# Graph attention on one core: sums per head on their own partitions, one copy a batch, PSUM operands for VectorE, more tiles gathered before the table, more rows fetched one by one, and a last batch in two parts

## The chip, the cores and the metric

The kernel runs on one core of a Trainium2 chip. The metric is the device time of one launch in microseconds (us), the median of three runs. Beside the runs stands one profiled execution, from which all rows of the trace come. Engines are named as in the profile: PE (TensorE), PEld (its weight loads), DVE (VectorE), ACT (ScalarE), POOL (GpSimd) and SP (SyncE, which here only starts DMAs). A letter q behind an engine (SPq, ACTq) is its queue of DMA issues and waits.

## The reference

12,500 nodes with 128 features, 412,500 edges sorted by their target. For each edge an attention value is made from the source row, the target row and 64 edge features; a softmax over the edges of a target (with a maximum that is at least 0, and a denominator that also counts the edges that do not go to this target) weighs the source rows, which are summed per target and added to x.

```python
h = relu(layernorm(x));  h = (h @ W_node.T).reshape(N, 4, 32);  e = (edge_attr @ W_edge.T).reshape(E, 4, 32)
att = sum(concat([h[src], h[tgt], e]) * a)             # per edge and head
att = where(att > 0, att, 0.2 * att)
m = maximum(segment_max(att, tgt), 0)
ex = exp(att - m[tgt])
denom = segment_sum(ex, tgt) + (E - deg) * exp(-m)
out = x + segment_sum(ex / denom[tgt] * h[src], tgt)   # summed over edges of a target
```

## The kernel before

**Preparation (to about 150 us).** 98 blocks of 128 nodes are normalised, projected by `wall` (128x144: per head 32 features, two ones and the source part of the attention; behind them four target parts) and written to a table in HBM (rows of 576 bytes). While that goes on, POOL gathers the source rows of the first edges from `x` itself, since the table is not there yet: these are the "raw" tiles, `RAW = (49, 9)`, all 49 of batch 0 and 9 of batch 1. They are normalised and projected in the same loop, three tiles a unit, behind the table's units. In the same loop the ranges of the targets are worked out (`chunk_ranges`), and ACT clears the accumulator `acc` in one copy (L453).

**Batches.** Edges go in tiles of 128, seven tiles a chunk (896 edges), seven chunks a batch (49 tiles), 66 batches; the last has six chunks, the last chunk three tiles. For each tile POOL issues an indirect DMA (L632) that gathers 128 rows of the table into `hs`, a ring of three buffers. From batch 5 on, the first tile of a batch (the first two where the batch number divides by `EVERY` = 4, none in the last batch) is not gathered by POOL but fetched row by row with DMAs of 576 bytes from the queues of SP (96 an iteration, or all that is left) and ACT (64): `by_row`, `row_by_row`, L658.

The order is written out by hand; engines run their own instructions in that order, and wait for each other by semaphores. Iteration b of the main loop holds: the loads of the next batches on SP (indices, the near target values `lw`, edge features `eft`, rows, penalties `pen`); `gather` of batch b+1 on POOL, behind a small memset `gate` (L627) that waits until the sums of batch b-2 have read the buffer; then on DVE `weigh(b)`, `mark(b)`, `scatter(b)`, the merge of the batches before (`close`), and `choose(b+1)`; on PE the sums of `scatter(b)` and then the edge part `z` of batch b+2 (`begin`, L691).

- `weigh` (L734 to L760): waits for the batch's rows, adds source and target parts, transposes to 32 partitions x 896, adds `z`, applies the slope 0.2 (L742, one instruction, both inputs the SBUF tile `att`), scans forward and back for the segment maximum (L745, L748), subtracts, and ACT takes the exponent (L752) while DVE makes four products of `pen` and `m` (L756).
- `mark` (L702 to L710): the 0/1 matrix `hot` (edge x 32 target slots).
- `scatter` (L774, L781): each chunk is multiplied with its weights (DVE, seven steps), and PE sums four chunks at a time: 128x128 stationary (four chunks' `hot` side by side), 502 columns moving, so the sums of a head land on the partitions of the chunk and not on those of the head. `collect` (L823) therefore copies 28 blocks of 32x35 a batch on ACT to where the merge wants them. The last batch takes `scatter_few` (L796: 128x32 stationary, 140 columns).
- `merge` (L829 to L869): two batches at a time (the last four singly) are joined by scans over chunks and added to `acc`, one iteration later. `finish` (L940 to L967) divides and stores a part of the nodes; inside the loop ACT moves its 16 blocks (L955), at the very end PE does (L957, 128x32 stationary at four column positions in turn).
- The last batch's rows are waited for in two steps (tiles 0 to 4, then 5 and 6): the steps up to the forward scan are done twice, everything behind it once for the whole batch, after the merge of the batch before.

Of the kernel before, what the change touches and what calls it, by code (L numbers as in the profile page):

```python
# [18 lines left out]
P = 128  # L19
N = 12500  # L20
D = 128
# [19 lines left out]
G = 4  # L41
RING = 3
AHEAD = 4
EARLY = 5
# [4 lines left out]
LOOSE = 4  # L49
RAW = (T * CB, XB)  # L50
# [7 lines left out]
SPLIT = 2 * AW  # L58
RUN = (G - 1) * ROW + SPLIT
# [9 lines left out]
SPROWS = 96  # L69
ACTROWS = 64  # L70
EVERY = 4
# [18 lines left out]
def by_row(b):  # L90

    return (2 if b % EVERY == 0 else 1) if LOOSE < b < NBT - 1 else 0
# [39 lines left out]
def kernel(  # L132
# [40 lines left out]
    acc = const.tile([P, NQ, AW], F32, name="acc")  # L173

# [6 lines left out]
    row_at = shared[P // 2:P // 2 + NBT - 3, :2 * P]  # L181
# [45 lines left out]
    with (  # L227
# [42 lines left out]
        wall = p1.tile([P, ROW], F32, name="wall")  # L270
# [34 lines left out]
        def load_rows(b0, n):  # L305
# [3 lines left out]
            if s.raw:  # L309
                k = int(b0 >= NB + RAW[0])  # L310
                i = b0 - NB - k * RAW[0]
                s.rows = raw[k][:, i:i + n, :]
# [99 lines left out]
        sizes += [min(XB, n - i) for n in RAW for i in range(0, n, XB)]  # L412
# [39 lines left out]
        def chunk_ranges():  # L452
            nc.scalar.copy(acc.rearrange("p q d -> p (q d)"), carry_m.to_broadcast([P, NQ * AW]))  # L453
# [260 lines left out]
    def weigh(s, before):  # L714
# [7 lines left out]
        zst = work.tile([P, T, R], F32, name="zst")  # L722
        att = work.tile([P, BUF], F32, name="a")[:R, :CE]
        up = ps.tile([P, BANKS * 512], F32, name="up")[:R, :CE]
        own = s.hs[:, :, :EROW].rearrange("p (t q) (h k) -> p t q h k", t=T, h=H)[:, :, :s.chunks, :, AW - 1]

        def grouped(what, g):
            return what.rearrange("r (t g i) -> r g t i", g=NQT, i=R)[:, g, :, :]

        for t0, t1 in ((0, EARLY), (EARLY, T)) if s.b == NBT - 1 else ((0, T),):  # L730
            if t0:
                landed(nc.vector, "late", late_sems, late_done, 0, s.hs[:, EARLY * CB:, :], s.ends[:, :, :, :])
            e0, e1 = t0 * P, t1 * P
            nc.vector.tensor_tensor(logits[:, t0:t1, :s.chunks * H].rearrange("p t (q h) -> p t q h", h=H),  # L734
                                    own[:, t0:t1], pick[:, t0:t1, :s.chunks, :H], op=OP.add)
            nc.vector.transpose(zst[:, t0:t1, :].rearrange("p t i -> p (t i)"),
                                logits[:, t0:t1, :].rearrange("p t i -> p (t i)"))
            for g in range(NQT):
                on_half(s, nc.vector.tensor_tensor(grouped(att, g)[:, t0:t1, :], grouped(s.z, g)[:, t0:t1, :],  # L739
                                                   zst[g * R:(g + 1) * R, t0:t1, :], op=OP.add))  # L740
            z = s.z[:, e0:e1]
            on_half(s, nc.vector.scalar_tensor_tensor(z, att[:, e0:e1], 0.2, att[:, e0:e1], op0=OP.mult, op1=OP.max))  # L742
            if before:
                collect(before, 0)
            on_half(s, nc.vector.tensor_tensor_scan(up[:, e0:e1], s.pen[:, e0:e1], z, up[:, e0 - 1:e0] if e0 else 0.0,  # L745
                                                    op0=OP.add, op1=OP.max))
        m = work.tile([P, BUF], F32, name="m")[:R, :CE]
        nc.vector.tensor_tensor_scan(m[:, ::-1], s.pen[:, CE:0:-1], up[:, ::-1], 0.0, op0=OP.add, op1=OP.max)  # L748
        on_half(s, nc.vector.tensor_tensor(att, s.z, m, op=OP.subtract))  # L749
        both = work.tile([P, 2, T, R], F32, name="both")  # L750
        for g in range(NQT):
            nc.scalar.activation(both[g * R:(g + 1) * R, 0, :, :], grouped(att, g), AF.Exp)  # L752
        if before:
            collect(before, 1)
# [576 lines left out]
```

## Time and profile before

| what | us |
|---|---|
| runs | 4022.22, 4022.31, 4023.95 (median 4022.31) |
| profiled execution | 4021.72, its span 4019.9 |
| POOL busy | 3010.7 (75%) |
| DVE busy | 2373.7 (59%) |
| PE busy | 1455.8 (36%) |
| ACT busy | 865.9 (22%) |

How to read it: the share of busy time says little by itself, since POOL's gathers are short instructions with a fixed pause between them that the page counts as idle time "issue" and not as work. The view of the groups by line gives busy time, the mean of one instruction, and what ended the idle time before them; the view of one line gives minimum, median and maximum; the timeline gives start and length of each instruction (several alike in a row are joined, "x28"), and in brackets the idle time before it. fp32 matmuls stand as two records each.

### The profile page before, as it was taken

The page shows a single profiled execution, that of the slowest core. Times are in us where ns is not written, and L with a number is a line of the kernel's source. Part 1 is how long each engine was busy: PE and PEld are TensorE (multiplying, and loading weights), DVE is VectorE, ACT ScalarE, POOL GpSimd, SP SyncE. Part 2 cuts the span into 40 slices and gives each one's busy share as a digit, 9 for nine tenths or more (in the row PEclk, how much of TensorE's full clock was granted, in tenths as well). Part 3 has the DMA queues.
Part 4 walks back from the last instruction along what each step waited for, and adds up shares of the span by engine and source line. Part 5 has one row for each costly group of instructions (what it writes and reads, how often), then busy time and mean ns, then how long its engine had stood idle before and what let it go on. Part 6 is the DMA issues. An engine that isn't in the chain of part 4 may idle for free.

```text
span 4019.9 us, 40260 instructions
## 1 busy us (share of the span) xinstructions
PE 1455.8 (36%) x3485; PEld 570.9 (14%) x3485; DVE 2373.7 (59%) x4282; ACT 865.9 (22%) x2682; POOL 3010.7 (75%) x3224
## 2 busy tenths in 40 slices
PE   5652432432442442442342442342342342343342
PEld 4320110110110110110110111110111110111111
DVE  7895565565565565465565565566465456465466
ACT  6321122112122112112122112122122122122122
POOL 6777777777777777777777777777777777777774
PEclk9776666766666666666666766676776676676676
DMA  7443333433333433433433433433334333434331
GB/s 214 130 134 109 100 96 108 110 89 99 107 91 108 110 94 99 110 87 105 109 97 95 110 88 106 108 104 88 110 89 110 104 108 85 109 89 109 109 93 42
DMA packets 283438, 418.03 MB, mean 104 GB/s; under 512 B 81019, under 2 KB 199862, under 8 KB 283146
## 3 DMA queue, kind: packets, MB, share of 16 engines
q0 software_dynamic: 100736, 231.80, 22.4%
q1 hardware_dynamic: 161232, 173.91, 14.5%
q10 hardware_dynamic: 21178, 9.69, 1.0%
q14 instruction: 262, 2.15, 0.2%
q8 instruction: 30, 0.49, 0.1%
HBM read 399.60 MB, written 15.51 MB: 103 GB/s over the span
## 4 chain that ended last, share of the span: by engine, by line
POOL 66%; issue 22%; DVE 7%; PE 3%; DMA 1%; ACT 1%; POOLq 0%; DVEq 0%; SPq 0%; ACTq 0%
POOL hs L632 66%; PE pa L781 1%; DVE hs L774 1%; PE z L691 1%; DVE stats L335 1%; DMA hs<-table,ends 1%; DVE hT L381 1%; DVE pick L607 1%; DVE m L748 0%; DVE up L745 0%; DVE hot L710 0%; DVE a L739 0%; ACT both L752 0%; DVE z L742 0%; DVE a L749 0%
## 5 line engine op out<-in xcount | busy, mean ns | idle before, releaser
L632 POOL DMA_INDIRECT hs<-table,ends x3090 | 2946.6, 954 | 945.0 <-issue 933.4
L781 PE MATMUL pa<-hs,hot 128*128 128x502 f32 x1820 | 924.6, 672 | 2428.0 <-DVE hs L774 2428.0
L734 DVE TENSOR_TENSOR logits<-hs,pick 128x196 f32<-128x196 f32 (+1 forms) x67 | 32.9, 491 | 1349.4 <-DVEq L666 1349.2
L781 PEld LDWEIGHTS pa<-hs,hot 128*128 128x128 f32 x1820 | 395.8, 222 | 2948.9 <-issue 2892.3
L823 ACT COPY r<-pa 32x35 f32<-32x35 f32 x1820 | 379.7, 209 | 1531.0 <-issue 1204.4
L774 DVE TENSOR_TENSOR hs<-hs,exr 128x924 f32<-128x924 f32 x455 | 472.5, 1110 | 0.0
L691 PE MATMUL z<-eft,wa 128*32 128x512 f32 (+3 forms) x1056 | 436.5, 549 | 13.5 <-DMA eft<-in_ef 13.5
L752 ACT ACTIVATE both<-a 32x224 f32<-32x224 f32 x264 | 102.4, 388 | 1153.1 <-DVE a L749 1150.7
L607 DVE COPY_PREDICATED pick<-exr,lw 128x3136 f32<-128x3136 int32 x66 | 239.8, 3633 | 0.0
L607 DVE COPY_PREDICATED pick<-exr,pick 128x1568 f32<-128x1568 int32 (+3 forms) x198 | 230.6, 1165 | 6.8
L590 ACT COPY pick<-lw 128x3136 f32<-128x3136 f32 x66 | 184.8, 2800 | 2.7 <-ACTq L666 1.2
L869 DVE TENSOR_TENSOR acc<-acc,a 128x70 f32 x461 | 107.2, 233 | 70.0 <-issue 51.2
L691 PEld LDWEIGHTS z<-eft,wa 128*32 128x32 f32 (+1 forms) x1056 | 94.6, 109 | 358.0 <-issue 350.7
L745 DVE TENSOR_TENSOR_SCAN up<-pen_sb,z 32x896 f32<-32x896 f32 x66 | 132.6, 2010 | 2.3
L748 DVE TENSOR_TENSOR_SCAN m<-pen_sb,up 32x896 f32<-32x896 f32 x66 | 132.5, 2007 | 2.3
L710 DVE TENSOR_TENSOR hot<-exr,key 128x448 f32<-128x448 f32 (+1 forms) x260 | 129.0, 559 | 6.7
L739 DVE TENSOR_TENSOR a<-z,zst 32x224 f32<-32x224 f32 (+2 forms) x268 | 101.0, 377 | 12.6 <-PE z L691 2.7
L756 DVE SCALAR_TENSOR_TENSOR both<-pen_sb,m 32x224 f32<-32x224 f32 x264 | 100.2, 380 | 2.7
L955 ACT COPY up<-a 32x224 f32<-32x224 f32 (+1 forms) x224 | 74.5, 332 | 36.0 <-DVE a L947 29.3
L742 DVE SCALAR_TENSOR_TENSOR z<-a 32x896 f32<-32x896 f32 (+1 forms) x67 | 72.1, 1076 | 2.3
L749 DVE TENSOR_TENSOR a<-z,m 32x896 f32<-32x896 f32 x66 | 71.3, 1080 | 2.3
L239 POOL DMA_INDIRECT hs<-in_x,ends x58 | 54.9, 947 | 18.1 <-issue 17.4
(166 smaller groups left out, 991.3 us busy)
## 6 DMA issues: line engine op xcount, KB each, us to landing
hs<-table SPq DMA_DIRECT2D x5760, 0.6 KB
eft<-in_ef SPq DMA_DIRECT2D x66, 1344.0 KB
hs<-table ACTq DMA_DIRECT2D x3840, 0.6 KB
hs<-table,ends POOLq DMA_INDIRECT x3090, 2.5
lw<-near SPq DMA_DIRECT2D x461, 64.0 KB
eft<-in_ef SPq DMA_DIRECT2D x66, 224.0 KB
pen_sb<-pens SPq DMA_DIRECT2D x66, 98.1 KB
table<-rows ACTq DMA_DIRECT2D x9, 648.0 KB
```

Source lines behind the costliest of these rows:

```text
L590: nc.scalar.copy(pick[:, :, :s.chunks, :], lw[:, None, :s.chunks, :n].to_broadcast([P, T, s.chunks, n]))
L607: nc.vector.copy_predicated(pick[:, :, :s.chunks, :n], bit[:, :, :, None].to_broadcast([P, T, s.chunks, n]), more)
L632: load = nc.gpsimd.indirect_dma_start(out=s.hs[:n, t * CB + q, :], out_offset=None, in_=table[:, :], in_offset=bass.IndirectOffsetOnAxis(a ...
L691: s.made = own_half(s, nc.tensor.matmul(s.z[:, part], wa3[:n, j, :], s.eft[:n, j, part], start=(j == 0), stop=(j == SB - 1)))
L710: nc.vector.tensor_tensor(s.hot[:, :, q0:q0 + n, :].rearrange("p t q r -> p q t r"), rows_ps[:, None, None, :].to_broadcast([P, n, T, W]), ...
L745: on_half(s, nc.vector.tensor_tensor_scan(up[:, e0:e1], s.pen[:, e0:e1], z, up[:, e0 - 1:e0] if e0 else 0.0, op0=OP.add, op1=OP.max))
L748: nc.vector.tensor_tensor_scan(m[:, ::-1], s.pen[:, CE:0:-1], up[:, ::-1], 0.0, op0=OP.add, op1=OP.max)
L752: nc.scalar.activation(both[g * R:(g + 1) * R, 0, :, :], grouped(att, g), AF.Exp)
L774: nc.vector.tensor_tensor(rows, rows, ex_ps[:, :, q * H:(q + 1) * H, None].to_broadcast([P, T, H, HB]), op=OP.mult)
L781: scattered[s.b] = nc.tensor.matmul(pa, s.hot[:, t, q0:q0 + G, :].rearrange("p q r -> p (q r)"), flat[:, at:at + RUN], start=(t == 0), sto ...
L823: nc.scalar.copy(to, pa[row:row + W, k:k + AW])
L869: nc.vector.tensor_tensor(cols, cols, put[:, i0 + i, :, :], op=OP.add)
```

## The change

1. *Sums.* Each chunk is multiplied and then summed at once, head by head: 28 matmuls a chunk (seven tiles, four heads), 128x32 stationary, 35 columns moving, the head choosing the column position (`tile_position=(0, h * W)`), so that a head's sums land on its own partitions. A batch has 196 matmuls in place of 14. `collect` is one copy of 128x245 a batch.
2. *Operands.* The sum with `z` is written to a PSUM tile `up`; the slope is two instructions (a product from `up` to SBUF, a maximum of `up` and that); the four products take the forward scan `up` (PSUM) in place of `m` (SBUF). The merge's `scale` and `put` lie in PSUM. `finish` always uses PE.
3. *Raw tiles.* `RAW[1]` goes from 9 to 18, so 67 tiles are gathered from `x`. The 18 of batch 1 are no longer processed in the preparation but in two new functions in iteration 0 (`measure_late`, `rows_late`), whose buffers lie in `acc` (`spare`); `acc` is therefore cleared in iteration 1.
4. *Rows.* `EVERY` 4 to 2, `LOOSE` 4 to 2, and the last batch takes part: 94 tiles row by row in place of 75. SP issues 112 an iteration (64 of them, if any of the next batch are left, ahead of the near values), ACT 80 (40 for batch 64, none for the last).
5. *End.* Batches 62 to 64 are merged in their own iteration, `mark` of 64 and 65 moves ahead, and the last batch is weighed, multiplied and summed in two parts (tiles 0 to 3, tiles 4 to 6; `EARLY` 5 to 4), whose sums are merged as twelve chunks.

```diff
-EARLY = 5
+EARLY = 4
-LOOSE = 4
-RAW = (T * CB, XB)
+LOOSE = 2
+RAW = (T * CB, 2 * XB)
-SPROWS = 96
-ACTROWS = 64
-EVERY = 4
+SPROWS = 112
+FRONT = 64
+ACTROWS = 80
+EVERY = 2
...
-    return (2 if b % EVERY == 0 else 1) if LOOSE < b < NBT - 1 else 0
+    return (2 if b % EVERY == 0 and b < NBT - 1 else 1) if LOOSE < b < NBT else 0
...
+def act_rows(b):
+    return ACTROWS if b < NBT - 2 else ACTROWS // 2 if b < NBT - 1 else 0
...
         def chunk_ranges():
-            nc.scalar.copy(acc.rearrange("p q d -> p (q d)"), carry_m.to_broadcast([P, NQ * AW]))
...
-                on_half(s, nc.vector.tensor_tensor(grouped(att, g)[:, t0:t1, :], grouped(s.z, g)[:, t0:t1, :],
-                                                   zst[g * R:(g + 1) * R, t0:t1, :], op=OP.add))
-            on_half(s, nc.vector.scalar_tensor_tensor(z, att[:, e0:e1], 0.2, att[:, e0:e1], op0=OP.mult, op1=OP.max))
+            on_half(s, nc.vector.tensor_tensor(grouped(up, g), grouped(s.z, g),
+                                               zst[g * R:(g + 1) * R, t0:t1, :], op=OP.add))
+        nc.vector.tensor_scalar(att[:, e0:e1], up[:, e0:e1], 0.2, None, op0=OP.mult)
+        on_half(s, nc.vector.tensor_tensor(z, up[:, e0:e1], att[:, e0:e1], op=OP.max))
...
-            nc.vector.scalar_tensor_tensor(both[g * R:(g + 1) * R, 1, :, :], grouped(s.pen[:, 1:], g), -1.0 / BIG,
-                                           grouped(m, g), op0=OP.mult, op1=OP.mult)
+            nc.vector.scalar_tensor_tensor(both[g * R:(g + 1) * R, 1, t0:t1, :], grouped(s.pen[:, 1:], g), -1.0 / BIG,
+                                           grouped(up, g), op0=OP.mult, op1=OP.mult)
...
+    def end_in_parts(s):
+        spans = ((0, EARLY), (EARLY, T))
...
+        for i, (t0, t1) in enumerate(spans):
+            if i:
                 landed(nc.vector, "late", late_sems, late_done, 0, s.hs[:, EARLY * CB:, :], s.ends[:, :, :, :])
+                weigh_part(s, t0, t1, None)
+            else:
+                weigh(s, None)
+            if i:
+                keep(i - 1)
+            pa = ps.tile([P, RUN], F32, name="pa", bufs=3)
+            sums.append(pa[:, :s.chunks * AW].rearrange("p (q d) -> p d q", d=AW))
+            for q in range(s.chunks):
...
+                multiply(s, q, t0, held)
+                add_up(s, pa, q, t0, held)
+        keep(len(spans) - 1)
+        return r, breaks
...
+    def add_up(s, pa, q, t0, t1):
+        for t in range(t0, t1):
+            for h in range(H):
+                scattered[s.b] = nc.tensor.matmul(
+                    pa[h * W:(h + 1) * W, q * AW:(q + 1) * AW], s.hot[:, t, q, :],
+                    s.hs[:, t * CB + q, h * AW:(h + 1) * AW],
+                    start=(t == t0), stop=(t == t1 - 1), tile_position=(0, h * W))
...
     def scatter(s):
+        pa = ps.tile([P, RUN], F32, name="pa", bufs=3)
+        s.sums = pa[:, :CB * AW].rearrange("p (q d) -> p d q", d=AW)
+        for q in range(CB):
+            multiply(s, q, 0, T)
+            add_up(s, pa, q, 0, T)
...
+        nc.scalar.copy(merged[first][0][:, :, at:at + CB], s.sums)
...
-                if by_act:
-                    nc.scalar.copy(po[s * W:(s + 1) * W, h // 2, h % 2, :n, :], w4[h * W:(h + 1) * W, :n, s, :])
-                    continue
...
+    def rows_late(s):
...
+        for u in range(n // XS + 1):
+            if u * XS < n:
+                hn = spare(XS * D).rearrange("p (i d) -> p i d", d=D)
...
+                for i in range(XS):
+                    nc.tensor.transpose(pt[:, i * P:(i + 1) * P], hn[:, i, :], ident)
+                turned[u] = spare(XS * P)
+                nc.vector.tensor_scalar(turned[u], pt, 0.0, None, op0=OP.max)
+            if u:
+                ph = both[:, 512:512 + XS * ROW].rearrange("p (i c) -> p i c", c=ROW)
+                for i in range(XS):
+                    nc.tensor.matmul(ph[:, i, :], turned[u - 1][:, i * P:(i + 1) * P], wall, start=True, stop=True)
+                rows = s.hs[:, (u - 1) * XS:u * XS, :]
+                nc.scalar.copy(rows, ph)
...
         begin(batch(1))
+        measure_late(batch(1))
         for b in range(NBT - 1):
...
-            before = batches[b - 1] if 1 <= b else None
+            before = batches[b - 1] if 1 <= b <= NBT - ALONE else None
+            soon = b >= NBT - ALONE
...
+            if b:
+                front = FRONT - row_by_row(batch(b + 1), nc.sync, ENG.SP, FRONT)
             load_near(batch(b + 1))
...
             scatter(s)
+            if b == 0:
+                rows_late(batch(1))
             spread(batch(b + 1))
...
+            if b == 1:
+                nc.scalar.copy(acc.rearrange("p q d -> p (q d)"), carry_m.to_broadcast([P, NQ * AW]))
+            if soon:
...
+                collect(s)
+                close(s)
...
-        weigh(s, None)
-        scatter(s)
-        close(before, NBT - 2)
-        for g in range(2):
-            collect(s, g)
-        close(s, NBT - 1)
+        merged[s.b] = end_in_parts(s)
+        close(s)
```

More of the change, by code (lines that the diff above doesn't have):

```diff
@@ L411 @@
         tables = len(sizes)
-        sizes += [min(XB, n - i) for n in RAW for i in range(0, n, XB)]
+        sizes += [min(XB, RAW[0] - i) for i in range(0, RAW[0], XB)]
         starts = [sum(sizes[:i]) for i in range(len(sizes))]
@@ L784, in scatter_few @@
[L784 to L797 removed]
+        open_weights(s)
@@ L1051 @@
                 counts = count_windows()
+            if b == 1:
+                nc.scalar.copy(acc.rearrange("p q d -> p (q d)"), carry_m.to_broadcast([P, NQ * AW]))
+            if soon:
+                for b0, n, behind in parts():
+                    if behind == b and not held_x:
+                        held_x[b0] = load_part(work, b0, n)
+                collect(s)
+                close(s)
             if b + 2 < NBT:
                 clear_rows(batch(b + 2))
[L1054 to L1055 removed]
+                row_by_row(batch(b + 2), nc.scalar, ENG.Activation, act_rows(b + 2))
+        s = batch(NBT - 1)
         for store in stores:
```

243 lines of the change are left out of this document (125 added, 118 removed).

## The prediction

> **What bounds the kernel now.** I read the page's busy times, then the chain that ended last, then the costliest groups, then the timelines of the beginning, of one batch and of the end.
>
> ```profile
> PE 1455.8 (36%) x3485; PEld 570.9 (14%) x3485; DVE 2373.7 (59%) x4282; ACT 865.9 (22%) x2682; POOL 3010.7 (75%) x3224
> ...
> POOL 66%; issue 22%; DVE 7%; PE 3%; DMA 1%; ACT 1%; POOLq 0%; DVEq 0%; SPq 0%; ACTq 0%
> ...
> L632 POOL DMA_INDIRECT hs<-table,ends x3090 | 2946.6, 954 | 945.0 <-issue 933.4
> ...
> hs<-table,ends POOLq DMA_INDIRECT x3090, 2.5
> ```
>
> The view of that one line adds minimum, median and maximum:
>
> ```profile
> L632 POOL DMA_INDIRECT hs<-table,ends x3090: 938/944/1822, 85.4 to 3973.5; - x194
> ```
>
> POOL is busy 75%, but 933.4 of its 945 us of idle time before gathers is "issue": 0.30 us behind each gather, waiting for nobody. A gather thus costs 0.944 + 0.304 = 1.248 us, and 3090 of them fill the time from 85.4 to 3974.4 without a hole. The chain says so too (POOL and issue 88%). What counts is the number of gathers, what lengthens them, when the first starts, and how much follows the last.
>
> ```profile
> 74.67 0.94 POOL L239 DMA_INDIRECT hs<-in_x,ends  x1 [0.30 <-issue]
> 85.41 0.94 POOL L632 DMA_INDIRECT hs<-table,ends  x1 [9.80 <-DMA table<-rows]
> ...
> 199.60 0.12 POOL L627 MEMSET gate<- 128x1 f32 x1
> ...
> 3973.46 0.95 POOL L632 DMA_INDIRECT hs<-table,ends  x1 [0.31 <-issue]
> ```
>
> The only hole is 9.8 us, in which POOL waits for the table. 85.41 + 3090 x 1.248 = 3941.7; the last gather ends at 3974.4, 32.7 later. The mean (954) lies 10 ns above the median (944), which is 31 us over 3090: some gathers are longer. Which ones:
>
> ```profile
> 196.89 1.47 POOL L632 DMA_INDIRECT hs<-table,ends  x1 [0.30 <-issue]
> ...
> 513.39 1.09 DVE L742 SCALAR_TENSOR_TENSOR z<-a 32x896 f32<-32x896 f32 x1
> 513.55 1.75 POOL L632 DMA_INDIRECT hs<-table,ends  x1 [0.30 <-issue]
> 514.52 2.02 DVE L745 TENSOR_TENSOR_SCAN up<-pen_sb,z 32x896 f32<-32x896 f32 x1
> 515.60 0.95 POOL L632 DMA_INDIRECT hs<-table,ends  x1 [0.30 <-issue]
> ...
> 3931.87 1.18 POOL L632 DMA_INDIRECT hs<-table,ends  x1 [0.30 <-issue]
> ```
>
> The gather at 513.55 starts while L742 runs (both inputs the SBUF tile `a`) and ends 0.8 us after L742, as if it began only then. The one at 515.60 starts under L745, whose second input `z` is PSUM, and keeps its length. Over the whole timeline 57 gathers end so behind an L742 (196.89 is the first, 3931.87 the last), 20.8 us longer in sum; 61 under L756 (`pen` and `m`, both SBUF) are longer by 3.8 us in sum.
>
> **Gathers.** The row-by-row tiles go from 75 to 94 and the raw tiles of batch 1 from 9 to 18: 3090 - 19 - 9 = 3062 gathers of the table. -28 x 1.248 = **-34.9 us**. The nine raw gathers go ahead of the table: 74.67 + 0.94 + 9 x 1.248 = 86.85, so the first table gather starts at about 87.15 in place of 85.41: **+1.7**. The hole of 9.8 us pays for the rest.
>
> **Lock.** L742 becomes a product (one PSUM input) and a maximum (`up` PSUM, `a` SBUF), L756 gets PSUM `up`. By L745 neither holds POOL up: **-24.6**. Bounds: 0 and all 31. DVE pays about 1.1 us a batch more (a second pass as long as L742).
>
> **Steady state.** One batch:
>
> ```profile
> 989.31 0.50 DVE L734 TENSOR_TENSOR logits<-hs,pick 128x196 f32<-128x196 f32 x1 [20.81 <-DVEq L666]
> ...
> 993.09 2.02 DVE L745 TENSOR_TENSOR_SCAN up<-pen_sb,z 32x896 f32<-32x896 f32 x1
> ...
> 1000.82 0.50 DVE L760 COPY hs<-zst 128x196 f32<-128x196 f32 x1
> ...
> 1003.69 7.27 DVE L774 TENSOR_TENSOR hs<-hs,exr 128x924 f32<-128x924 f32 x7
> 1004.41 24.35 ACTq L658 DMA_DIRECT2D hs<-table  x64
> ...
> 1008.14 14.33 PE L781 MATMUL pa<-hs,hot 128*128 128x502 f32 x28 [41.22 <-DVE hs L774]
> ...
> 1022.40 6.55 PE L691 MATMUL z<-eft,wa 128*32 128x512 f32 x16
> ...
> 2885.22 3.31 SPq L581 DMA_DIRECT2D lw<-near  x7
> ...
> 2892.13 35.76 SPq L658 DMA_DIRECT2D hs<-table  x96
> ```
>
> DVE waits 20.8 us for the gather; the new period is 47.5 x 1.248 = 59.3 us. The lower rows of SP are of another batch. SP's rows take 0.374 us each, ACT's 0.38: 112 and 80 an iteration make 42 and 30 us. For SP's other issues (3.3 us for the near values, and features, penalties, indices and the pauses for register loads, such as the 3.6 us from 2888.53 to 2892.13) I take 11 us, so SP has 6 us to spare a batch; the 64 rows put ahead of the near values push these back by some 23 us, onto ACT's copy a period later. The one copy in place of 28 saves ACT some 5 us that nobody waits for. All this I cost at 0; the cover is the POOL period.
>
> **PE.** 196 matmuls are 392 records. Two rows price them:
>
> ```profile
> L957 PEld LDWEIGHTS up<-a,ident x32: 128/177/178, 4009.0 to 4010.4; 128*32 128x32 f32 x32
> L957 PE MATMUL up<-a,ident x32: 394/421/423, 4009.1 to 4010.6; 128*32 128x128 f32 x32
> L796 PE MATMUL pa<-hs,eft x76: 282/283/442, 3987.7 to 3996.8; 128*32 128x140 f32 x76
> ```
>
> L957 walks the four column positions as the new sums do: 31 steps in 1.5 us, 47 ns a record, loads of 177 ns overlapping. L796 stays on one position for a chunk: 75 steps in 9.1 us, 0.12. I take 47, the same form: 18.4 us a batch, begun after one multiplication (1.04 us) in place of four, so the sums end about when they did; bound 0.12, 47 us. The section "Part 3: Packing small matmuls — row/col tiling" of the Trainium skill's page "TensorE: Matmul & The Clock Gate" says that a weight load overlaps matmuls in flight only when the row groups differ; here only the columns differ. By that rule the pairs would run one behind the other, which is the rival below (4067 us); L957's loads, 177 ns long and 45 ns apart, speak against it.
>
> **Beginning.** `gate` of batch 3 waits for batch 0's sums.
>
> ```profile
> 86.19 11.63 ACT L453 COPY acc<-carry_m 128x13720 f32<-128x13720 f32 x1
> ...
> 99.26 0.27 DVE L335 BATCH_NORM_STATS2 stats<-hs 128x6 f32<-128x128 f32 x1 [4.71 <-issue]
> ...
> 130.10 0.55 DVE L381 TENSOR_SCALAR hT<-pt 128x384 f32<-128x384 f32 x1
> ...
> 147.40 0.53 DVE L381 TENSOR_SCALAR hT<-pt 128x384 f32<-128x384 f32 x1 [0.81 <-PE pt L376]
> ...
> 149.15 0.41 SPq L572 DMA_DIRECT2D eft<-in_ef  x1
> ...
> 164.27 1.55 DVE L739 TENSOR_TENSOR a<-z,zst 32x224 f32<-32x224 f32 x4 [2.68 <-PE z L691]
> ...
> 177.56 1.11 DVE L774 TENSOR_TENSOR hs<-hs,exr 128x924 f32<-128x924 f32 x1
> ```
>
> The preparation loses three units (12 units from 130.10 to 147.40, 1.57 us each: 4.7) and the clearing of `acc`, for which DVE stood 4.7 us: 9.4 earlier. `measure_late` (18 steps of 0.2 us and 0.8) takes 4.5, of which the wait for `z` hides 2.7. L739 then starts at 156.7, the multiplications at 156.7 + 13.3 + 1.1 = 171.1, the sums at 172.2, done at 190.6. POOL reaches the gate at 87.15 + 80 x 1.248 = 187.0, and 1.5 of lengthening (199.6 before, 3.1 above 85.41 + 89 x 1.248): it waits **+2** (bounds 0 and 15: the preparation might lose only the three units, and then wait). `rows_late` (six units of some 2 us) follows on PE and delays batch 1's weights to about 216 and its sums to 252; POOL wants those at 190.6 + 48 x 1.248 = 250.5: within a microsecond or two, in the bound. ACT's clearing and 80 rows delay batch 2's exponents to about 268, its sums to 290; POOL wants them at 309.
>
> **End.**
>
> ```profile
> 3928.51 0.50 DVE L734 TENSOR_TENSOR logits<-hs,pick 128x196 f32<-128x196 f32 x1 [18.97 <-DVEq L666]
> ...
> 3963.78 0.20 DVE L594 TENSOR_TENSOR away<-ends,floor 128x49 int32<-128x49 int32 x1
> ...
> 3973.38 0.23 DVE L734 TENSOR_TENSOR logits<-hs,pick 128x120 f32<-128x120 f32 x1
> ...
> 3976.22 1.49 DVE L745 TENSOR_TENSOR_SCAN up<-pen_sb,z 32x640 f32<-32x640 f32 x1
> ...
> 4000.98 0.17 DVE L834 TENSOR_SCALAR mc<-pick 128x6 f32<-128x6 f32 x1 [1.97 <-ACT pick L823]
> ...
> 4007.21 0.17 DVE L942 TENSOR_SCALAR rest<-acc 128x16 f32<-128x16 f32 x1
> ```
>
> Before, 45.5 us follow the last gather's end (3974.4 to 4019.9). After, counted from the start of batch 64's weights (0; before 3928.51, and the last gather ends 45.9 later with 38 gathers, 44.65 with 37): weights 12.0 + 1.1, multiplications to 20.4, choose and mark of 65 (9.6 from 3963.78 to 3973.38) to 30.0; PE sums from 14.3 to 32.7, copy 33.3, merge 6.7 to 40 (6.2 from 4000.98 to 4007.21 for six chunks), small steps 40.8. Part one: the steps to the scan took 4.3 us for five tiles (3973.38 to 3977.71) and 5.8 for seven (989.31 to 995.11), so twelve us for seven become 7.4 + 0.6 for four: 48.8; six multiplications of at most 0.68: 3.9 more. Part two is landed by then (44.65 and 2.5): 5.8 + 0.5, so 59.0; PE is free of part one (184 records, 8.7 us) at 58.3 and sums 120 records until 65.5; copy 0.7, merge of twelve 7.2 (6.2 and longer scans), 12.7 from 4007.21 to the end: 86.1. That is 41.5 behind the last gather: **-4.0** (bounds -9, with merges half hidden, and +8, with PE at 60 ns and longer PSUM steps).
>
> **Sum.** The profiled execution took 4021.7 (span 4019.9; the median of the runs is 0.6 above it): 4021.7 - 34.9 + 1.7 - 24.6 + 2 - 4 = 3961.9, say **3962**.
>
> **Rivals.**
> - *Column positions do not overlap* (the other side). At 0.12 us a record the sums take 47 us. Batch 0's end at 219, 29 us behind what POOL wants; `rows_late` and batch 1's weights follow, and its sums end some 27 us late again; the steady state still holds (47 + 6.6 of 59.3). At the end batch 64's merge waits 29 longer, and the two parts' sums add 20: 3962 + 29 + 27 + 49 = 4067. L957 speaks against it, its 32 records being few speaks for it. From 90 ns a record on it decides.
> - *The lock stays* (the new maximum or product holds POOL as L742 did): 3962 + 24.6 = 3986. Against it: L745 and L748.
> - *The beginning stands*: gates wait 15 to 20 us more: 3980.
> - *Rows come late, the tiles taken off POOL are waited for on DVE*: SP must fall from 0.374 to over 0.43 us a row before its queue is longer than the period; at 0.45 it loses some 2 us a batch, 3962 + 130 = 4090. No row of SP is that slow.
>
> **How the numbers follow.** The forecast (3946 to 3975) has 0.74, the lock 0.07, the beginning 0.08, the columns 0.08, late rows 0.03. The range 3946 to 3988 leaves out the columns and the rows, 11 in 100, and some 6 for errors in the sizes. Within 0.2% (8 us, what these runs can tell from no change) only a half-sized columns case would land: 0.02. Faster 0.88, slower 0.10.
>
> **What will show it.** 3062 gathers with a mean of 946 to 947 ns, from about 87 to 3918 to 3920; no gather ending behind the new slope; the sums' 392 records a batch in 18 to 20 us; ACT's copies one a batch; the wait at `gate` of batch 3 a few us; 41 to 42 us behind the last gather. Wrong it would be by a PE group near 45 us a batch, by gathers still over 950 ns on average, or by DVE's idle time moving from the gather to rows (the same wait, with SP busy to its end).

## Result and profile after

The changed kernel takes 3959.16 us (median of 4 executions, 3958.09 to 3961.07), the kernel before on the same chip 4022.26: a ratio of 0.9843, 95% interval 0.9826 to 0.986. It is 1.6% faster, and 2.8 us below the 3962 that was forecast. The profiled execution took 3959.01 us, its span 3957.2.

In the first set of experiments (e1 to e4) every execution, the kernel before's too (6465.75 us), took some 1.6 times as long, and in the last set (e9 to e12) some ran 0.3% longer in everything (a median gather of 947 ns in place of 944), so times are given as ratios to the kernel before of the same set, and from the first set mainly its traces are read.

First the page's busy times, its chain and its costliest group, then the view of the gathers' line (minimum, median and maximum in ns, first and last start in us):

```profile
PE 1117.2 (28%) x27848; PEld 633.7 (16%) x27848; DVE 2455.3 (62%) x4386; ACT 432.1 (11%) x693; POOL 2969.7 (75%) x3205
...
POOL 63%; issue 21%; DVE 6%; PE 1%; SPq 1%; DMA 1%; ACT 0%; DVEq 0%; POOLq 0%; ACTq 0%
...
L639 POOL DMA_INDIRECT hs<-table,ends x3062 | 2897.1, 946 | 927.2 <-issue 925.4
```

```profile
L639 POOL DMA_INDIRECT hs<-table,ends x3062: 940/944/1970, 87.0 to 3917.0; - x192
```

The bound is the one of before: POOL and its pause behind each gather. There are 28 gathers fewer, and their mean has come down from 954 to 946 ns at the same median of 944. The timeline of POOL at the beginning, at the first gate and at the end:

```profile
85.55 0.94 POOL L249 DMA_INDIRECT hs<-in_x,ends  x1 [0.30 <-issue]
86.99 0.94 POOL L639 DMA_INDIRECT hs<-table,ends  x1 [0.50 <-issue]
...
189.19 0.12 POOL L634 MEMSET gate<- 128x1 f32 x1
189.50 0.94 POOL L639 DMA_INDIRECT hs<-table,ends  x1 [0.19 <-ACT acc L1028]
...
3917.00 0.94 POOL L639 DMA_INDIRECT hs<-table,ends  x1 [0.30 <-issue]
```

The hole of 9.8 us ahead of the table is filled with raw gathers, the gate holds nothing up, and behind the last gather (3917.00 + 0.94) 39.3 us are left of the span. So the 62.7 us between the two spans (4019.9 and 3957.2) come apart like this:

| part | forecast | measured | from |
|---|---|---|---|
| 28 gathers fewer | -34.9 | -34.9 | 3062 for 3090, 1.248 each |
| first table gather later | +1.7 | +1.6 | 86.99 for 85.41 |
| gathers no longer lengthened | -24.6 | -23.1 | gathers over 974 ns: 145 with 30.7 us too many before, 45 with 7.6 after |
| gate of batch 3 | +2 | 0 | 189.19 |
| end | -4.0 | -6.2 | 39.3 for 45.5 |
| sum | -59.8 | -62.6 | 62.7 between the spans |

### The profile page after: what moved, and what is told of

Its sections match the earlier page's. It is cut to its first block, busy times and chain, and to the rows that moved or that the text cites. A ratio compares the mean times of both kernels' runs of the same rounds, so it can differ in the third digit from the quotient of the medians.

```text
span 3957.2 us, 91934 instructions
## 1 busy us (share of the span) xinstructions
PE 1117.2 (28%) x27848; PEld 633.7 (16%) x27848; DVE 2455.3 (62%) x4386; ACT 432.1 (11%) x693; POOL 2969.7 (75%) x3205
## 4 chain that ended last, share of the span: by engine, by line
POOL 63%; issue 21%; DVE 6%; PE 1%; SPq 1%; DMA 1%; ACT 0%; DVEq 0%; POOLq 0%; ACTq 0%
POOL hs L639 63%; SPq L665 1%; DVE hs L814 1%; PE pa L821 1%; DMA hs<-table,ends 1%; DVE pick L614 1%; DVE up L759 0%; DVE m L761 0%; DVE acc L894 0%; PE z L698 0%; DVE up L754 0%; DVE hot L717 0%; PE up L979 0%; SPq L661 0%; DMA up<-in_dstc 0%
## 5 line engine op out<-in xcount | busy, mean ns | idle before, releaser
L821 PE MATMUL pa<-hs,hot 128*32 128x35 f32 x25480 | 473.3, 243 | 2505.9 <-DVE hs L814 2240.4
L821 PEld LDWEIGHTS pa<-hs,hot 128*32 128x32 f32 x25480 | 419.2, 149 | 2595.7 <-issue 2499.8
L749 DVE TENSOR_TENSOR logits<-hs,pick 128x196 f32<-128x196 f32 (+1 forms) x67 | 33.0, 493 | 1046.0 <-DVEq L673 1006.6
L814 DVE TENSOR_TENSOR hs<-hs,exr 128x924 f32<-128x924 f32 (+2 forms) x466 | 478.5, 1097 | 0.0
L764 ACT ACTIVATE both<-a 32x224 f32<-32x224 f32 (+2 forms) x268 | 103.2, 385 | 2798.6 <-DVE a L762 2550.8
L894 DVE TENSOR_TENSOR acc<-acc,up 128x70 f32 x461 | 105.1, 228 | 90.2 <-issue 55.4
L759 DVE TENSOR_TENSOR_SCAN up<-pen_sb,z 32x896 f32<-32x896 f32 (+1 forms) x67 | 133.3, 1990 | 15.4 <-DMA pen_sb<-pens 13.1
L761 DVE TENSOR_TENSOR_SCAN m<-pen_sb,up 32x896 f32<-32x896 f32 (+1 forms) x67 | 132.6, 1979 | 2.3
L754 DVE TENSOR_TENSOR up<-z,zst 32x224 f32<-32x224 f32 (+2 forms) x268 | 103.2, 385 | 12.8
L768 DVE SCALAR_TENSOR_TENSOR both<-pen_sb,up 32x224 f32<-32x224 f32 (+2 forms) x268 | 100.0, 373 | 3.8
L758 DVE TENSOR_TENSOR z<-up,a 32x896 f32<-32x896 f32 (+1 forms) x67 | 72.0, 1075 | 2.3
```

What stands on the lines that cost most here:

```text
L754: on_half(s, nc.vector.tensor_tensor(grouped(up, g), grouped(s.z, g), zst[g * R:(g + 1) * R, t0:t1, :], op=OP.add))
L761: nc.vector.tensor_tensor_scan(mp[:, ::-1], s.pen[:, e1:e0:-1], up[:, e0:e1][:, ::-1], 0.0, op0=OP.add, op1=OP.max)
L764: nc.scalar.activation(both[g * R:(g + 1) * R, 0, t0:t1, :], grouped(att, g), AF.Exp)
L814: nc.vector.tensor_tensor(rows, rows, ex_ps[:, t0:t1, q * H:(q + 1) * H, None].to_broadcast([P, t1 - t0, H, HB]), op=OP.mult)
L821: scattered[s.b] = nc.tensor.matmul(pa[h * W:(h + 1) * W, q * AW:(q + 1) * AW], s.hot[:, t, q, :], s.hs[:, t * CB + q, h * AW:(h + 1) * AW ...
L894: nc.vector.tensor_tensor(cols, cols, put[:, i0 + i, :, :], op=OP.add)
```

## Experiments

**The slope's operands.** Four kernels ask whether it was the operands' place that held POOL up. e1 makes only this edit in the kernel before:

```
-                on_half(s, nc.vector.tensor_tensor(grouped(att, g)[:, t0:t1, :], grouped(s.z, g)[:, t0:t1, :],
+                on_half(s, nc.vector.tensor_tensor(grouped(up, g)[:, t0:t1, :], grouped(s.z, g)[:, t0:t1, :],
...
-            on_half(s, nc.vector.scalar_tensor_tensor(z, att[:, e0:e1], 0.2, att[:, e0:e1], op0=OP.mult, op1=OP.max))
+            nc.vector.tensor_scalar(att[:, e0:e1], up[:, e0:e1], 0.2, None, op0=OP.mult)
+            on_half(s, nc.vector.tensor_tensor(z, up[:, e0:e1], att[:, e0:e1], op=OP.max))
```

> The kernel before, with only the slope's step changed as the change does it: the sum of z and zst goes to the PSUM tile `up`, a product (one PSUM input) and a maximum (one PSUM input, one SBUF input) take the place of the one step with two SBUF inputs. Rows, raw tiles, sums and the end stay. Theory (two SBUF inputs hold POOL up): no gather ends behind the slope any more, the 3090 gathers' mean falls from 954 to 947 ns, 20.8 us go: 4022.3 - 20.8 + 1 at the end = about 4002.5, ratio 0.995. Rival (the lengthening comes from something else that the change removed, the copies of ACT or SP's rows): the mean stays at 954, time 4022 to 4024.

In the first set its gathers had a mean of 946 ns, and none ended behind the slope. Its ratio was 1.0058, but POOL was not the bound in that set (see the rows below), so its time does not decide. Run again:

> The kernel of e1 once more (the kernel before, with the slope's product and maximum reading PSUM and nothing else of the change), where a row costs SP the 0.375 us of the kernel before's trace. Theory (two SBUF inputs hold POOL up): mean of the 3090 gathers 946 to 947 ns, 20 to 25 us less than before: 4022 - 21 + 1 = 4002, ratio 0.995. Rival (POOL's shorter gathers are given back as waits, since the 1.1 us a batch on DVE or the gates take their place): 4018 to 4024.

Measured: ratio 0.9948 (0.9932 to 0.9965), 20.9 us of 4022, and 14 to 27 by the interval. The gathers' group in e10:

```profile
L632 POOL DMA_INDIRECT hs<-table,ends x3090 | 2925.1, 947 | 945.1 <-issue 934.2 <-DMA table<-rows 9.7 <-PE z L691 0.6
```

The number of gathers and the wait for the table are those of before, and the 954 has become 947. The gathers' time falls by 21.5 us (2946.6 to 2925.1) and the span by 18.9 (4019.9 to 4001.0): 2.4 us come back behind the last gather, where 48.0 us follow in place of 45.5. So the part is worth nearly what the trace of before had added up behind L742.

e2 is the reverse: the changed kernel with the slope in one step from `a`.

```
-            on_half(s, nc.vector.tensor_tensor(grouped(up, g), grouped(s.z, g),
+            on_half(s, nc.vector.tensor_tensor(grouped(att, g), grouped(s.z, g),
...
-        nc.vector.tensor_scalar(att[:, e0:e1], up[:, e0:e1], 0.2, None, op0=OP.mult)
-        on_half(s, nc.vector.tensor_tensor(z, up[:, e0:e1], att[:, e0:e1], op=OP.max))
+        on_half(s, nc.vector.scalar_tensor_tensor(z, att[:, e0:e1], 0.2, att[:, e0:e1], op0=OP.mult, op1=OP.max))
```

> The changed kernel with the slope's step as before: one step with both inputs from the SBUF tile `a`; all else of the change stays. Both theories of the lock: some 57 gathers end behind this step again, 20 us in sum; DVE is one pass shorter (1.1 us a batch, of which some 1.2 to 2.3 us count at the end): 3959.2 + 20 - 2 = about 3977, mean of the gathers 952 to 953 ns. Rival (no lock without ACT's 28 copies a batch): 3957.

In the first set the mean was 954 ns, with 36 gathers behind the slope's step. Run again:

> The kernel of e2 once more (the changed kernel with the slope as one step, both inputs the SBUF tile `a`). Theory: some 57 gathers end behind that step, 20 us in sum, DVE one pass shorter in the end: 3959 + 20 - 2 = 3977, mean of the gathers 952 to 953 ns. Rival (the longer gathers are absorbed by slack elsewhere): 3957 to 3961.

Measured: ratio 0.9892 (0.9875 to 0.9908), which is 0.0049 or 20 us above the changed kernel's, with intervals that do not meet. Of e11's gathers, the view of the line and the group:

```profile
L639 POOL DMA_INDIRECT hs<-table,ends x3062: 943/947/1972, 87.0 to 3952.3; - x192
```

```profile
L639 POOL DMA_INDIRECT hs<-table,ends x3062 | 2931.3, 957 | 928.1 <-issue 927.1 <-DVEq L888 0.3 <-DMA eft<-in_ef 0.3
```

The mean stands 10 ns above its median again, as before the change, and 57 gathers end behind the slope's step, 27.2 us longer in sum. ACT's 28 copies a batch are not in this kernel, so they were not what lengthened the gathers.

e3 keeps two steps but takes both from SBUF, which tells the form of the instruction from the place of its inputs:

```
-            on_half(s, nc.vector.tensor_tensor(grouped(up, g), grouped(s.z, g),
+            on_half(s, nc.vector.tensor_tensor(grouped(att, g), grouped(s.z, g),
...
-        nc.vector.tensor_scalar(att[:, e0:e1], up[:, e0:e1], 0.2, None, op0=OP.mult)
-        on_half(s, nc.vector.tensor_tensor(z, up[:, e0:e1], att[:, e0:e1], op=OP.max))
+        nc.vector.tensor_scalar(m[:, e0:e1], att[:, e0:e1], 0.2, None, op0=OP.mult)
+        on_half(s, nc.vector.tensor_tensor(z, att[:, e0:e1], m[:, e0:e1], op=OP.max))
```

> The changed kernel with the slope's two steps on SBUF tiles: product from `a` to `m`, both SBUF, then the maximum of `a` and `m`, both SBUF. Theory (any DVE step of this length whose two inputs are both in SBUF holds POOL up): the maximum lengthens gathers by some 20 us in sum, as the one step did; the product has one input and lengthens none, unless it runs in half its time (0.55 us in place of 1.08): 3979. Rival (it is the form scalar_tensor_tensor that holds POOL up, not where its inputs lie): 3959 with a mean of 946. Second rival (a product from SBUF to SBUF holds POOL up too): two groups of long gathers, 30 to 40 us, 3990 to 4000.

Two stretches of e3's timeline:

```profile
431.26 0.61 DVE L757 TENSOR_SCALAR m<-a 32x896 f32<-32x896 f32 x1
431.45 1.25 POOL L639 DMA_INDIRECT hs<-table,ends  x1 [0.30 <-issue]
...
1053.65 1.09 DVE L758 TENSOR_TENSOR z<-a,m 32x896 f32<-32x896 f32 x1
1053.74 3.50 SPq L665 DMA_DIRECT2D hs<-table  x2
1053.75 0.14 PEld L698 LDWEIGHTS z<-eft,wa 64*32 64x32 f32 x2 [0.62 <-issue]
1054.04 1.51 POOL L639 DMA_INDIRECT hs<-table,ends  x1 [0.30 <-issue]
```

The gather that starts under the maximum ends 0.81 us behind it, and the one that starts under the product ends 0.83 us behind that: the mechanism of the second rival. The form does not matter: tensor_tensor holds POOL up as scalar_tensor_tensor did. And the product does it too, with one input only, once that input is in SBUF; it then runs in 0.61 us, where the changed kernel's, from PSUM, takes 1.08. Over the trace, 22 gathers started under the product and 21 under the maximum and were lengthened, by 16.2 us in sum. This was seen in the first set alone. e3 was not run in a second one, so the 30 to 40 us of that rival are not shown. The Trainium skill says of this, on the page "SBUF — State Buffer" in the section "Who interferes with whom", that a DVE instruction with two SBUF inputs gets in the way of a GpSimd instruction that reads SBUF, and that a tensor_scalar in the double-rate mode takes the shared ports for its whole length. The gathers agree in both, with 0.81 and 0.83 us. On the page "VectorE: DVE Perf Modes", section "Why PSUM operands drop a tier", the Trainium skill says that a PSUM operand keeps fp32 at the single rate; 1.08 against 0.61 us agrees. The slower product from PSUM costs DVE 0.47 us, and no gather ends behind it.

**The order of the sums.** e4 computes the same 392 records a batch, seven of one column position in a row in place of an alternation record by record:

```
-        for t in range(t0, t1):
-            for h in range(H):
+        for h in range(H):
+            for t in range(t0, t1):
                 scattered[s.b] = nc.tensor.matmul(
```

> The changed kernel with the same 392 matmul records a batch in another order: for each chunk all seven tiles of one head (one column position) and then the next head, where the change alternates the four positions record by record. Theory (records overlap only with records of another column position; 0.12 us each on one position, as L796 of before): some 0.1 us a record, 40 us a batch in place of 14; the steady state hides it, the beginning waits some 20 us at the gate of batch 3 and the end 30 to 50 us: 4010 to 4030. Rival (neighbouring records overlap on one position as well): sums of 14 to 15 us a batch, 3959 within 4 us.

In the first set's trace the 392 records of a batch took some 12 us in the median. Run again:

> The kernel of e4 once more (seven records of one column position, then the next position). Its trace of e4 showed 392 records in 11.3 to 12.5 us without a pause, 30 ns a record, not the 0.1 us that the theory of e4 had. New theory (records of this size, 35 columns, cost 30 ns on one position; PE's instructions arrive in blocks of 128 pairs some 3.5 us apart, so the order of the change, 19 ns a record, waits between blocks and is done no sooner): sums of 11 to 13 us a batch, 3959 within 3 us. The theory of e4 still: 4010 to 4030.

Measured: ratio 0.9834 (0.9817 to 0.985), span 3956.4: no difference from the change. A batch's sums in the changed kernel, and one in e12:

```profile
2942.04 4.11 PE L821 MATMUL pa<-hs,hot 128*32 128x35 f32 x210 [35.45 <-DVE hs L814]
2946.89 1.99 PE L821 MATMUL pa<-hs,hot 128*32 128x35 f32 x128 [0.74 <-issue]
2950.37 0.68 PE L821 MATMUL pa<-hs,hot 128*32 128x35 f32 x54 [1.49 <-issue]
```

```profile
1040.61 12.06 PE L821 MATMUL pa<-hs,hot 128*32 128x35 f32 x392 [39.86 <-DVE hs L814]
```

What a record costs depends on the granted clock, the share of PE's full speed that the profile gives for each stretch; here it was 0.50 up to 1045.4 us in e12 and up to 2946.6 in the changed kernel, and 1.00 from there to the end of the batch. In e12 a record costs 44 ns at 0.50 (110 of them in 4.79 us) and 25 at 1.00 (the other 282). Alternating, it costs 20 ns at 0.50 (4.11 / 210) and 16 at 1.00 (1.99 / 128), but the alternating ones stop for 0.7 to 1.5 us after blocks of 128. From its first record to its last a batch of 392 takes 8.7 to 15.0 us in the changed kernel, 9.6 in the median, and 11.2 to 18.6 in e12, 12.2 in the median. So the alternation is done sooner, which the expectation of e12 did not have, but nothing waits for the difference. Neither 47 ns nor 0.12 us is the price, and the rival that hung on 0.09 us a record is gone with both orders.

**Gathers against rows.** e6 takes the row-by-row tiles back to the 75 of before:

```
-    return (2 if b % EVERY == 0 and b < NBT - 1 else 1) if LOOSE < b < NBT else 0
+    return (2 if b % 4 == 0 else 1) if 4 < b < NBT - 1 else 0
```

> The changed kernel with the row-by-row tiles of before (75 in place of 94); all else of the change stays. Theory: 19 gathers more, 19 x 1.248 = 23.7 us: 3983. Rival (the extra rows cost something on SP, ACT or the DMA engines that lengthens the gathers or a wait): less than 23.7, say 3965 to 3975.

Measured: 3980.47 us, ratio 0.9895 (0.9878 to 0.9911), 21.3 above the change. e6 has 3081 gathers, and 19 of them are 23.7 us, so all but some 2 us of that arrived; its interval does not tell 21.3 from 23.7. In its trace the lengthened gathers come to 5.6 us in place of 7.6, and 37.8 us follow the last gather in place of 39.3. The shorter end is not the rows' doing, since e8 (below) has it too with the rows of the change.

e5 goes on in the other direction:

```
-SPROWS = 112
+SPROWS = 120
...
-ACTROWS = 80
+ACTROWS = 104
...
-    return (2 if b % EVERY == 0 and b < NBT - 1 else 1) if LOOSE < b < NBT else 0
+    return (2 if b % 4 and b < NBT - 1 else 1) if LOOSE < b < NBT else 0
```

> The changed kernel with more row-by-row tiles: two in three batches of four and one in the fourth (109 in all, where the change has 94), ACT's share 104 rows a batch and SP's 120. Theory (POOL's number of gathers sets the time while the row queues fit into the period of about 58.7 us): about 15 gathers fewer, 15 x 1.248 = 18.7 us less: 3940. Rival (rows come late: SP needs 120 x 0.375 + 11 = 56 us, close to the period, and ACT 104 x 0.38 + 7 = 46.5 us): DVE waits for rows in place of gathers, no gain or a loss, 3955 to 3990.

Measured: 3943.53 us, ratio 0.9803 (0.9786 to 0.9819): 15.6 faster than the change, of 18.7. Two waits of DVE, in the changed kernel and in e5 (total us, times, longest):

```profile
DVE logits L749 <- DVEq L673: 1006.6, 55, 29.3
...
DVE exr L770 <- ACT both L764: 47.6, 38, 7.8
```

```profile
DVE exr L770 <- ACT both L764: 551.9, 65, 18.4
...
DVE logits L749 <- DVEq L673: 360.3, 31, 29.3
```

DVE's wait for gathers has gone from 1006.6 to 360.3, and its wait for ACT's exponentials, which stand behind 104 rows in ACT's queue, from 47.6 to 551.9. POOL is still the bound, but the slack that covers the rows is going. Of the 3.1 us that did not arrive, 1.5 lie at the first gather of the table (88.46 us in place of 86.99), and POOL pauses for 1.60 and 1.38 us before two gathers, in place of 0.30, for a reason that the trace does not name. By these waits it is ACT's queue, with the exponentials behind its rows, that a further step of this kind would meet; that was not run.

What dear rows do can be read in the first set. Of e4, a line of SP's timeline and the page's chain that ended last:

```profile
3002.92 97.23 SPq L665 DMA_DIRECT2D hs<-table  x112
```

```profile
SPq 41%; issue 33%; ACTq 10%; DVE 5%; another core or an unknown queue 4%; ACT 1%; DMA 1%; PE 0%; DVEq 0%
```

There a row costs SP 0.87 us (97.23 / 112), twice the 0.43 from which the prediction has SP's queue longer than the period, and the chain lies on the queues that issue rows and no longer on POOL. e1, with the 75 row-by-row tiles of before, stood at 1.006 of the kernel before, and e2 to e4, with 94, at 1.076 to 1.083. So this is the rival of late rows at work: with such rows the tiles taken off POOL cost time. That the 19 tiles make up the whole difference was not tried, and why a row took so long in that set stays open.

e8 takes nine of the raw tiles back:

```
-RAW = (T * CB, 2 * XB)
+RAW = (T * CB, XB)
```

> The changed kernel with 9 raw tiles of batch 1 in place of 18. Theory: nine more gathers of the table, 9 x 1.248 = 11.2 us, which start 1.4 to 1.6 us earlier: +9.7, 3969. Rival (the 18 tiles' later work on DVE, PE and ACT costs time at the gates of the first batches, which 9 tiles don't): less, 3960 to 3965.

Measured: 3967.44 us, ratio 0.9861 (0.9844 to 0.9877), 8.3 above the change. The timeline of e8 has the hole again:

```profile
74.49 0.94 POOL L249 DMA_INDIRECT hs<-in_x,ends  x1 [0.30 <-issue]
86.40 0.94 POOL L639 DMA_INDIRECT hs<-table,ends  x1 [10.96 <-DMA table<-rows]
```

Nine gathers more (11.2) start 0.6 earlier, and its end is 1.5 shorter. POOL waits at no gate in either trace, so the later preparation of the 18 tiles costs no time that can be seen; the measured 8.3 lies between the theory's 9.7 and the rival's 6 at most, and its interval does not tell them apart.

**The last batch.** e7 computes it in one part:

```
-EARLY = 4
+EARLY = T
...
-        spans = ((0, EARLY), (EARLY, T))
...
-        for i, (t0, t1) in enumerate(spans):
...
+        weigh(s, None)
+        pa = ps.tile([P, RUN], F32, name="pa", bufs=3)
+        for q in range(s.chunks):
+            multiply(s, q, 0, tiles_of(s.c0 + q))
+            add_up(s, pa, q, 0, tiles_of(s.c0 + q))
+        nc.scalar.copy(r[:, :, 1:], pa[:, :s.chunks * AW].rearrange("p (q d) -> p d q", d=AW))
```

> The changed kernel with its last batch in one part: all its gathers are waited for, then weights of seven tiles, six multiplications, sums, one copy, a merge of six chunks. Theory: DVE starts the weights at about 3920.6 in place of 3911.4, weights 13.3, multiplications 6.2, last sums 1, copy 0.4, merge 6.2, from there 12.7: 3920.6 + 39.8 = 3960.4 against a span of 3957.2, +3 us: 3962. Rival (the parts' second weights, second sums and the merge of twelve cost what the earlier start saves): 3957 to 3960.

Measured: 3964.25 us, ratio 0.9853 (0.9837 to 0.987), 5.1 above the change; the intervals overlap, so the trace has to say it. DVE's wait for the gather in e7, and the start of part one in the changed kernel:

```profile
3921.87 0.46 DVE L749 TENSOR_TENSOR logits<-hs,pick 128x168 f32<-128x168 f32 x1 [8.21 <-DVEq L673]
```

```profile
3911.36 0.32 DVE L749 TENSOR_TENSOR logits<-hs,pick 128x96 f32<-128x96 f32 x1 [0.21 <-DVEq L673]
```

In one part DVE stands for 8.2 us, then needs 42.9 to the end of the span (3964.8); in two parts it stands for 0.2 and needs 45.8. The second set of steps costs 2.9, the wait saved is 8.0: 5 us. Behind the end of the last gather 44.9 us follow in e7, for 39.3.

e9 is e5 with the last batch's differences and marks put ahead of batch 64's weights (`differ` holds the first three steps of `choose`):

```
+            if b == NBT - 2:
+                differ(batch(b + 1))
+                mark(batch(b + 1))
             weigh(s, before)
...
-            if b >= NBT - 3:
+            if b == NBT - 3:
                 mark(batch(b + 1))
```

> The kernel of e5 (109 row-by-row tiles; 3943.5) with the last batch's differences and marks made before batch 64's weights, in the 3.7 us in which DVE waited there for the gather in e5, in place of behind its multiplications. Theory (from that wait on DVE is the chain to the end): 0.75 + 2.2 us less, 3940.5. Rival (the last gather's landing, or batch 64's rows, end the wait in its place): no gain, 3943 to 3945.

Measured: 3950.71 us in a set in which the kernel before took 4034.62, ratio 0.9794 (0.9778 to 0.981). That does not tell it from e5. The start of batch 64's weights in e5 and in e9:

```profile
3858.06 0.50 DVE L749 TENSOR_TENSOR logits<-hs,pick 128x196 f32<-128x196 f32 x1 [3.70 <-DVEq L673]
```

```profile
3867.56 0.50 DVE L754 TENSOR_TENSOR logits<-hs,pick 128x196 f32<-128x196 f32 x1 [0.86 <-DVEq L678]
```

From there to the end of the span it is 83.2 us in e5 (3941.3) and 80.3 in e9 (3947.9): the 2.9 that the moved steps take. The wait has shrunk from 3.70 to 0.86 us; this part holds in the trace, and its worth in time is not shown. e5 and e9 both beat the changed kernel: their intervals end below where its begins.

## Why the prediction was right

**Gathers.** Right to the count, 3062, and to 0.2 us in the start, 86.99 where the prediction had 87.15. e6, e5 and e8 move the number by +19, -15 and +9, and the time by +21.3, -15.6 and +8.3.

**Lock.** Right in mechanism (e10, e11) and nearly in size, 23.1 of 24.6. Nothing in the trace ends behind the new product or maximum. Of the 7.6 us that stay, 2.4 lie in the preparation before 140 us and about as much under L749, whose inputs are both in SBUF. The rival of a lock that stays is refuted; e3 shows that it would have come true had the two steps read SBUF.

**Steady state.** Right: POOL waits at no gate, and one copy a batch, 0.38 us, stands on ACT where 28 did; no run with rows at 0.375 us lost time to rows that came late, as far as its trace shows. The 3.6 us that the prediction puts down to pauses hold two issues of `eft` of 0.39 and 0.52 us, which changes nothing in it. The cover was there for the rows, and e5 shows how much of it was left. It hung on the price of a row: the rival of late rows, against which the prediction had that no row of SP is that slow, is what bounds e4 in the first set, at 0.87 us a row.

**PE.** The step "I take 47, the same form: 18.4 us a batch" failed, to the safe side. L957's records move 128 columns and the new ones 35, so the form was not the same: at the same granted clock of 0.50, L957's cost 47 ns and the new ones 20. The bound of 0.12 was a mean over two clocks: where the position stays the same, L796's records start 233 ns apart at 0.50 and 119 at 1.00, and e12's 59 and 31. That is some 1.7 and 0.9 ns a column at both widths, so on one position the price goes with the columns moved. L957's 47 ns are a mean as well: four records, one on each position, start within 20 ns, and the next four 213 ns after the first, which is 1.7 ns a column again. So the four positions do work side by side.

The rule of the Trainium skill cited there (a weight load overlaps matmuls in flight only across row groups) would have made pairs follow one another. Both orders of the sums keep to one row group. In e12's trace a weight load is 106 ns long at the least, and on one column position the next pair still begins 31 ns later at the full clock, so by these records the loads overlap the matmuls before them, and the trace disagrees with the rule.

**Beginning.** Forecast +2, measured 0. The timeline of the changed kernel around batch 0's sums:

```profile
154.23 0.50 DVE L749 TENSOR_TENSOR logits<-hs,pick 128x196 f32<-128x196 f32 x1
...
169.77 7.26 DVE L814 TENSOR_TENSOR hs<-hs,exr 128x924 f32<-128x924 f32 x7
...
177.46 0.54 DVE L1025 TENSOR_SCALAR acc<-hs,acc 128x128 f32<-128x128 f32 x1
...
207.53 0.18 DVE L601 TENSOR_TENSOR away<-ends,floor 128x49 int32<-128x49 int32 x1 [2.38 <-issue]
...
218.14 0.50 DVE L749 TENSOR_TENSOR logits<-hs,pick 128x196 f32<-128x196 f32 x1 [0.30 <-DVEq L673]
```

```profile
183.44 1.04 PE L821 MATMUL pa<-hs,hot 128*32 128x35 f32 x55 [1.69 <-issue]
...
244.75 0.28 PE L821 MATMUL pa<-hs,hot 128*32 128x35 f32 x9 [1.14 <-issue]
```

The multiplications begin at 169.8 (forecast 171.1), the sums end at 184.5 (190.6), and POOL reaches the gate at 189.2 (188.5 by 187.0 and the lengthening): the 2 us of wait were the over-priced sums. Another step was wrong and cost nothing: `rows_late` takes DVE from 177.5 to 207.5, not some 12 us, since each unit goes from ACT to PE to DVE and back with little overlap. The choosing for batch 1 waits for it, yet batch 1's weights begin at 218.1 (216 forecast), and its sums end at 245.0, ahead of the 249.4 at which POOL comes to the next gate (250.5 forecast). The slow step and the quick sums cancelled, which is luck: begun at 234.8 and 18.4 long, as forecast, the sums would have held POOL up by some 4 us.

**End.** Forecast 41.5 behind the last gather, measured 39.3. Its course in the changed kernel (DVE, then PE):

```profile
3873.55 0.50 DVE L749 TENSOR_TENSOR logits<-hs,pick 128x196 f32<-128x196 f32 x1 [7.29 <-DVEq L673]
...
3903.31 0.17 DVE L859 TENSOR_SCALAR mc<-r 128x7 f32<-128x7 f32 x1
...
3923.69 0.27 DVE L749 TENSOR_TENSOR logits<-hs,pick 128x72 f32<-128x72 f32 x1
...
3931.15 2.46 DVE L814 TENSOR_TENSOR hs<-hs,exr 128x396 f32<-128x396 f32 x5
...
3944.49 0.17 DVE L967 TENSOR_SCALAR rest<-acc 128x16 f32<-128x16 f32 x1
```

```profile
3895.95 1.67 PE L821 MATMUL pa<-hs,hot 128*32 128x35 f32 x96 [2.16 <-issue]
...
3935.43 0.50 PE L821 MATMUL pa<-hs,eft 128*32 128x35 f32 x17 [1.43 <-issue]
```

Counted from 3873.55, the step that failed is "PE sums from 14.3 to 32.7, copy 33.3": they end at 24.1, and the merge of batch 64 begins at 29.8, right behind choosing and marking. That is 3.5 earlier. Part two is waited for by nobody; its weights run from 50.1 to 57.6, 7.5 us where 6.3 were reckoned, and the sums end at 62.4 (65.5). The 12.7 us of the rest came out as they were (3944.49 to 3957.2). The sizes of PE's records account for both parts of the error of the sum, 2 at the gate and 2.2 here; the lock's 1.5 stands against them.

## What to carry to other kernels

Where a POOL that issues one gather after another is the bound, look for gathers that end a fixed time behind a DVE instruction, and give that instruction a PSUM input: it may run longer on DVE and still pay. Count what a moved load costs on the queue that takes it, and look at what stands behind it in that queue; here fifteen gathers more could be moved, and brought 15.6 of their 18.7 us, while the wait for the exponentials grew tenfold. Such a trade holds at one price of a row: with rows at 0.87 in place of 0.375 us, e2 to e4 were 8% slower than the kernel before. A small matmul is priced from a record of its own width at the same granted clock, not from one of its form.

## What the runs showed of the hardware

PE's instructions themselves can be late. The sums of the changed kernel stop after each 128 records, with "issue" as the only cause; the page's instruction queue of before and after:

```profile
q8 instruction: 30, 0.49, 0.1%
```

```profile
q8 instruction: 220, 3.60, 0.4%
```

220 packets of 16.4 KB for 27848 pairs are 127 pairs a packet, which is the length of the blocks. From block to block it takes some 3.5 us (2946.89 to 2950.37), 27 ns a pair, so pairs that run in 16 to 20 ns wait for their instructions. Over the whole trace 74 of the 75 times that two stops of over 0.4 us fall into one batch they are 128 records apart, and only one batch has no such stop; in e12, whose records cost 25 to 44 ns, 53 of 66 batches have none. The Trainium skill has the blocks, on the page "Runtime: NRT & Kernel Launch", section "Instruction fetch mechanics": 16 KiB with 256 instructions each. The Trainium skill also says there that the fetching is hidden behind the issue of instructions; for these small records the trace disagrees, with stops of 0.7 to 1.5 us in the batch shown. That the stops are the fetching was read from these counts, not tried by an experiment of its own.

And a gather held up by DVE does not share time with it. Whatever the moment at which it starts under the step, it ends some 0.8 us behind the step's end (0.81 and 0.83 in e3, 0.8 before the change). By these numbers a step of 1.09 us lengthens a gather that starts with it by an estimated 1.09 + 0.81 - 0.94 = 0.96 us, and one that starts 0.96 later not at all. The two forms differ for a gather that has already begun: none that began 0.12 to 0.9 us ahead of L742 was longer, but 16 that began 0.24 to 0.45 us ahead of e3's product were, and each ended 0.12 us behind the product.
